# LayerNorm scaling in two routed FFNs: from VectorE to GpSimd

## The chip, the cores and the metric

The kernel runs on one core of one Trainium2 chip. The metric is the device time of one execution in microseconds (us). Engines are named as the profile names them: PE is TensorE's matmul (PEld its weight load), DVE is VectorE, ACT is ScalarE, POOL is GpSimd, SP is SyncE, which here only starts DMAs.

## What is computed

The input is x of shape (2, 4096, 512) in float32: two sequences of 4096 tokens. A block of the model is an FFN, an attention and the same FFN again, each on the LayerNorm of x and each added to x:

```
x = x + 0.5 * ffn(layernorm(x))
x = x + attn(layernorm(x))
x = x + 0.5 * ffn(layernorm(x))

def _layernorm(x, axis=-1, eps=1e-05):
    m = jnp.mean(x, axis=axis, keepdims=True)
    v = jnp.var(x, axis=axis, keepdims=True)
    return (x - m) / jnp.sqrt(v + eps)
```

The FFN is a routing over 64 slots. Every token gets 64 logits from a hidden layer of 256 (gelu), keeps the 8 largest, and their softmax is its weight `alpha` on the slots. The slots gather the tokens with these weights, a GRU cell changes them, and each token reads the slots back with the same weights:

```
h = gelu(ctx @ w1.T + b1);  route_logits = (h @ w2.T + b2) / (abs(tau) + 0.1)
topk_vals, topk_idx = top_k(route_logits, 8);  topk_w = softmax(topk_vals)
slot_input = einsum('bts,btd->bsd', alpha, x);  slot_wsum = alpha.sum(axis=1) + 1e-08
... GRU of slot_input / slot_wsum, linear map wv ...
out = einsum('bts,bsd->btd', alpha, slot_values) @ wo.T + bo
```

The attention is a gated delta rule over 16 heads of 32, with a scan over the tokens. It is not touched here.

## The kernel before

The work is cut into 32 blocks. A block is 128 tokens of both sequences, so one tile of 128 partitions by 2 x 512. The program has five stages one after another: the routing of the first FFN, its GRU, the attention (with the first FFN's read-back in it), the routing of the second FFN, and then its GRU and read-back, which writes the output.

A routing (`ffn_a_phase`, L309) goes over groups of four blocks, with a group of one at the beginning and groups of two and one at the end (`split_blocks`, L53), ten groups in all. Each group passes through six generators. `a_load` starts the DMAs of the token tiles on SP. `a_stats` (L355) takes bn_stats (L361) and bn_aggr (L362) of each half tile on DVE, and the root and reciprocal for the scale (L365 on ACT, L366 on DVE). `a_norm` (L368) makes the normalized tile `xn` (L379, two instructions a block), casts it to float16 on ACT (`xh`, L383), and takes the rest of the split, `xl = xn - xh`, on POOL (L385). PE then transposes both (L394), ACT and DVE copy the transposes from PSUM (L397, L399). `a_hidden` does the hidden layer in three float16 matmuls (`mm3`, L128 to L130), gelu on ACT (L417) and the logits on PE (L421). `a_topk` (L425) is a sequence on DVE for a whole group: L431, the eight largest (L436), their removal (L439), L441, the exponential on ACT (L442), L444, L447, L448, L451, and the split of `alpha` (L457, L458); POOL adds `alpha` to a running sum, `wacc` (L461). `a_slots` transposes `alpha` (L472, L475) and adds up the slots on PE (L482 to L484), reading `xh` and `xl` from the buffers of L380 and L381.

The buffers around the change: `xn` has 2 in each FFN (`CFG`, `XN`), so a block's scaling reuses the buffer of the block two before, which L383 and L385 must have read. `xh` and `xl` have 10 in the first FFN and 11 in the second (`XH`). The first routing has work besides: the weights of the attention are scaled and split (`setup_attention`, L253, with L158, L159, L176 and L177), and a part of the GRU is done ahead (`setup_gh`, L231, L248).

`run_merged` (L60) draws the generators' pieces in the order of their due times (`PA`, L1079), and outside the attention the framework's scheduler then sets the order of each engine's queue. So an instruction that changes its engine can shift others. The attention runs under a written order (`PIPE`, L1081, within `manual_schedule`). Every engine works through its queue in order; a waiting instruction holds all that stand behind it. GpSimd's queue holds, in a routing, only L385, L461, a memset and the last sums of `wacc` (L338).

Of the kernel before, what the change touches and what calls it, by code (L numbers as in the profile page):

```python
# [14 lines left out]
ALU = mybir.AluOpType  # L15
# [79 lines left out]
def tile_macaron(  # L95
# [7 lines left out]
    nc = tc.nc  # L103
    V = nc.vector
# [204 lines left out]
    def ffn_a_phase(load, adst, nm, extra, before=None, after=None):  # L309

        with tc.tile_pool(name=f"sl{nm}", bufs=1, space=PSUM) as slp, tc.tile_pool(name=f"gp{nm}", bufs=1) as gp:
# [3 lines left out]
            with tc.tile_pool(name=f"f{nm}", bufs=2) as wp, tc.tile_pool(name=f"fs{nm}", bufs=2) as sm, \  # L315
                    tc.tile_pool(name=f"ft{nm}", bufs=3, space=PSUM) as ptr, \
                    tc.tile_pool(name=f"fp{nm}", bufs=2, space=PSUM) as ppj, \
                    tc.tile_pool(name=f"fl{nm}", bufs=2, space=PSUM) as ppl:
                groups = split_blocks(NBLK)
                ng = len(groups)  # L320
                pools = (wp, sm, ptr, ppj, ppl)
                st = [dict() for _ in range(ng)]
                items = []
                for g, (b0, n) in enumerate(groups):
                    args = (st[g], nm, g, (b0, n), pools)
                    t0, t1 = b0 / GB, (b0 + n) / GB
                    items += [
                        (t0 - PA["ld"] - n / GB, t1 - PA["ld"] - n / GB, lambda a=args: a_load(*a, load)),
                        (t0 - PA["st"], t0 - PA["st"] + PA["std"], lambda a=args: a_stats(*a)),
                        (t0, t1, lambda a=args: a_norm(*a)),  # L330
                        (t0 + PA["a2"], t1 + PA["a2"], lambda a=args: a_hidden(*a)),
                        (t1 + PA["a2"], t1 + PA["tk"], lambda a=args: a_topk(*a, wacc)),
                        (t1 + PA["tk"], t1 + PA["tk"] + PA["sl"] * n / GB, lambda a=args: a_slots(*a, adst, sl, ng)),
                    ]
                items += extra(gp, ptr, gw, NBLK / GB)
                run_merged(items)
                for i in range(1, GB):
                    nc.gpsimd.tensor_tensor(wacc[:, 0:NB], wacc[:, 0:NB], wacc[:, NB * i:NB * i + NB], ALU.add)  # L338
# [29 lines left out]
    def a_norm(d, nm, gi, blocks, pools):  # L368

        wp, sm, ptr, ppj, ppl = pools  # L370
        mv, rs = d["mv"], d["rs"]
        d["xhl"], d["xT"] = [], []
        for j in range(blocks[1]):
            u = f"{nm}{gi}_{j}"
            xs = d["x"][j]
            xn = wp.tile([P, NB, D], F32, tag="xn", name=f"fxn{u}", bufs=CFG[nm]["XN"])
            for b in range(NB):
                i = NB * j + b
                V.tensor_scalar(xn[:, b], xs[:, b], mv[:, i, 0:1], rs[:, i:i + 1], ALU.subtract, ALU.mult)  # L379
            xh = wp.tile([P, NB, D], F16, tag="xh16", name=f"xh{u}", bufs=CFG[nm]["XH"])  # L380
            xl = wp.tile([P, NB, D], F16, tag="xl16", name=f"xl{u}", bufs=CFG[nm]["XH"])  # L381
            d["xhl"].append((xh, xl))
            nc.scalar.copy(xh, xn)  # L383
            yield (j + 0.2) / blocks[1]
            nc.gpsimd.tensor_tensor(xl, xn, xh, ALU.subtract)  # L385
            yield (j + 0.4) / blocks[1]
            xTh = wp.tile([P, KC, NB * P], F16, tag="xTh", name=f"fxTh{u}", bufs=3)
            xTl = wp.tile([P, KC, NB * P], F16, tag="xTl", name=f"fxTl{u}", bufs=3)
            d["xT"].append((xTh, xTl))
            for src16, dst, eng in ((xh, xTh, 0), (xl, xTl, 1)):  # L390
                pt = ptr.tile([P, KC, NB * P], F16, tag="tr", name=f"fpt{u}_{eng}")
                for k in range(KC):
                    for b in range(NB):
                        nc.tensor.transpose(pt[:, k, b * P:(b + 1) * P], src16[:, b, k * P:(k + 1) * P], ident16)  # L394
                    yield (j + 0.4 + 0.3 * eng + 0.07 * (k + 1)) / blocks[1]
                if eng == 0:
                    nc.scalar.copy(dst, pt)  # L397
                else:
                    V.tensor_copy(dst, pt)  # L399
                yield (j + 0.7 + 0.3 * eng) / blocks[1]  # L400
# [751 lines left out]
```

## Time and profile before

| | |
|---|---|
| Median of 3 runs | 2361.86 us (2361.6 to 2366.88) |
| The profiled execution, its own time | 2367.99 us |
| Its span, first to last instruction | 2366.2 us |
| Mean granted TensorE clock | 0.952 |
| Busy share of the span | PE 89%, PEld 67%, DVE 81%, ACT 48%, POOL 34% |
| First routing, about | 20 to 262 us |
| Second routing, about | 2036 to 2262 us |

A row of the profile's groups gives the line, the engine, the operation, the tiles written and read, their sizes, the count, the busy time in us, the mean of one in ns, and the idle time of the engine just before them with what ended it. The shares above are means over stages with different limits, so the stages are read apart. Tile names end in the FFN's letter: `fxna` is `xn` in the first, `fxnc` in the second. `kx` and `xt` are both token tiles of the second FFN (14 of 32 are kept in SBUF for the read-back).

### The profile page before, as it was taken

Reading aid. Unit: us, or ns where it says so; the run is one execution under the profiler, and the core shown is the slowest. Engines: PE = TensorE matmul, PEld = TensorE weight load, DVE = VectorE, ACT = ScalarE, POOL = GpSimd, SP = SyncE. Lnnn points to the kernel's source line nnn. Section 1 sums busy time; section 2 is a strip of 40 time slices with the busy share of each in tenths; the row PEclk is TensorE's granted clock in tenths of the full one; section 3 lists DMA queues with packets and bytes.
Section 4 is the critical chain, followed back from the end, with each engine's and each line's share of the span. In section 5 each row is a group of like instructions: output and inputs, shape, how many; then the busy total and the mean of one; then the engine's idle time right before and its main releaser. Section 6 shows DMA issues by size and latency. Waiting matters only on the chain.

```text
span 2366.2 us, 101086 instructions
## 1 busy us (share of the span) xinstructions
PE 2113.8 (89%) x44989; PEld 1595.9 (67%) x44989; DVE 1920.3 (81%) x4876; ACT 1134.2 (48%) x1924; POOL 807.7 (34%) x750
## 2 busy tenths in 40 slices
PE   5778879999999999999999999999999976588985
PEld 5667847767777676766767677777667754477863
DVE  7898547988888888888888888888888885797664
ACT  4677445544445444444544444554444521467620
POOL 3333114433334333334434333433333441244200
PEclk9998889999999999999999999999999987789986
DMA  6332323344434344443334344344334332621069
GB/s 215 117 126 90 94 85 130 117 134 130 147 125 129 123 135 131 136 136 116 124 126 140 127 142 135 124 128 138 122 125 147 100 91 69 234 97 59 22 238 342
DMA packets 185444, 310.10 MB, mean 131 GB/s; under 512 B 28976, under 2 KB 82736, under 8 KB 185008
## 3 DMA queue, kind: packets, MB, share of 16 engines
q1 hardware_dynamic: 167600, 260.12, 33.1%
q10 hardware_dynamic: 17408, 43.52, 5.6%
q8 instruction: 352, 5.77, 1.2%
q14 instruction: 84, 0.69, 0.1%
HBM read 192.38 MB, written 111.20 MB: 128 GB/s over the span
## 4 chain that ended last, share of the span: by engine, by line
PE 57%; DVE 13%; DMA 10%; issue 3%; ACT 1%; SPq 1%; POOL 1%; DVEq 0%; ACTq 0%; POOLq 0%
PE apo L1064 9%; PE pa L943 5%; PE pv L128 5%; PE pc L1019 5%; DMA kd<-qk 4%; PE pc L1002 4%; PE pv L129 4%; PE pv L130 4%; PE pq L128 4%; PE pq L129 3%; PE pq L130 3%; PE pc L1012 3%; DMA x1r<-x1d 3%; PE kqt L853 2%; DVE fxnc L379 1%
## 5 line engine op out<-in xcount | busy, mean ns | idle before, releaser
L1064 PE MATMUL apo<-wo,Gt 128*128 128x512 f32 x512 | 281.1, 634 | 28.4 <-DVE x1r L1067 28.3
L128 PE MATMUL pv<-xTh,wgh 128*128 128x256 f16 x1024 | 282.3, 276 | 0.1
L129 PE MATMUL pv<-xTh,wgl 128*128 128x256 f16 x1024 | 280.4, 274 | 0.4 <-issue 0.4
L130 PE MATMUL pv<-xTl,wgh 128*128 128x256 f16 x1024 | 280.5, 274 | 0.0
L998 POOL TENSOR_TENSOR ps<-ST,AC 128x256 f32<-128x256 f32 x128 | 105.4, 823 | 457.2 <-DVE ST L1022 457.0
L128 PE MATMUL pq<-wqh,xTh 128*128 128x384 f16 (+1 forms) x768 | 243.4, 317 | 1.6 <-issue 0.9
L129 PE MATMUL pq<-wqh,xTl 128*128 128x384 f16 (+1 forms) x768 | 241.4, 314 | 0.2 <-DVE xTl L802 0.2
L130 PE MATMUL pq<-wql,xTh 128*128 128x384 f16 (+1 forms) x768 | 241.3, 314 | 0.0
L846 POOL TENSOR_TENSOR qk<-qk,rn 128x512 f32<-128x512 f32 x128 | 138.0, 1079 | 232.9 <-issue 107.3
L820 ACT ACTIVATE qk<-pq,iscA 128x384 f32<-128x384 f32 (+1 forms) x192 | 105.2, 548 | 164.4 <-PE pq L130 141.5
L964 POOL TENSOR_TENSOR KQ<-KQ,Ax 128x512 f32<-128x512 f32 x128 | 168.1, 1313 | 0.8 <-PE pa L943 0.8
L748 DVE TENSOR_TENSOR tmp<-N,MT 128x256 f32<-128x256 f32 (+7 forms) x384 | 162.3, 429 | 5.6
L742 DVE TENSOR_TENSOR tmp<-N,U 128x256 f32<-128x256 f32 (+7 forms) x384 | 164.7, 436 | 1.4
L822 ACT ACTIVATE sq<-pq,iscA 128x384 f32<-128x384 f32 (+1 forms) x192 | 164.8, 858 | 0.0
L1002 PEld LDWEIGHTS pc<-KQ,S 32*32 32x32 f32 x8192 | 123.5, 106 | 51.5 <-ACT Y L1028 31.4
L744 DVE TENSOR_REDUCE MT<-tmp 128x32 f32<-128x256 f32 (+7 forms) x384 | 153.6, 407 | 0.0
L943 PE MATMUL pa<-KQ 32*32 32x64 f32 x8192 | 143.4, 217 | 11.1 <-ACT KQ L856 5.0
L1002 PE MATMUL pc<-KQ,S 32*32 32x64 f32 x8192 | 142.8, 217 | 9.9 <-DVE S L1024 4.5
L1019 PEld LDWEIGHTS pc<-X,u 32*32 32x32 f32 x8192 | 121.9, 106 | 38.2 <-issue 21.1
L1019 PE MATMUL pc<-X,u 32*32 32x64 f32 x8192 | 143.1, 218 | 4.8 <-ACT u L1016 3.5
L943 PEld LDWEIGHTS pa<-KQ 32*32 32x32 f32 x8192 | 121.8, 106 | 37.6 <-issue 14.7
L750 DVE TENSOR_REDUCE N<-tmp 128x32 f32<-128x128 f32 (+4 forms) x320 | 135.3, 423 | 0.0
(303 smaller groups left out, 5728.7 us busy)
## 6 DMA issues: line engine op xcount, KB each, us to landing
d<-a0d ACTq DMA_DIRECT2D x32, 528.0 KB
Ax<-a0d ACTq DMA_DIRECT2D x32, 528.0 KB
xt<-in_x_dram SPq DMA_DIRECT2D x32, 512.0 KB
x<-in_x_dram SPq DMA_DIRECT2D x64, 256.0 KB
x1d<-x SPq DMA_DIRECT2D x64, 256.0 KB
vtd<-vg SPq DMA_DIRECT2D x64, 256.0 KB
kd<-qk SPq DMA_DIRECT2D x64, 256.0 KB
XK<-kd SPq DMA_DIRECT2D x256, 64.0 KB
```

Source lines behind the costliest of these rows:

```text
L128: nc.tensor.matmul(po, lh, rh, start=start, stop=False, skip_group_check=True)
L129: nc.tensor.matmul(po, ll, rh, start=False, stop=False, skip_group_check=True)
L130: nc.tensor.matmul(po, lh, rl, start=False, stop=stop, skip_group_check=True)
L742: V.tensor_tensor(tv, vw(f, o10 + j0, [[C, n], [0, h], [1, ni]]), vw(U, ou + j0 * 17, [[0, n], [16, h], [1, ni]]), ALU.mult)
L744: yield lambda tv=tv, j0=j0: V.tensor_reduce(vw(mt, n * j0, [[1, n], [n, h]]), tv, AX.X, ALU.add)
L748: V.tensor_tensor(tv, vw(f, o11 + r0 * C, [[C, h], [0, n], [1, nk]]), vw(mt, 0, [[0, h], [n, n], [1, nk]]), ALU.mult)
L822: nc.scalar.activation(sq[:, f0:f1].rearrange("p (q g e) -> p q e g", g=NG, e=C), pq[:, 0:f1 - f0].rearrange("p (q e g) -> p q e g", g=NG, ...
L943: nc.tensor.matmul(pa[s, m], KQ[s, 0, c, b, g], KQ[s, :, c, b, g], start=(m == 0), stop=True, skip_group_check=True, tile_position=(32 * q ...
L964: nc.gpsimd.tensor_tensor(kc, kc, bass.AP(Ax.tensor, Ax[:, :, c].offset, [list(a[0]), [1, 2], list(a[1]), [1, C]]), ALU.mult)
L1002: nc.tensor.matmul(pcv[s, b, g, 0:2 * C], S[s, b, g], KQ[s, :, c, b, g], start=(g == 0), stop=False, skip_group_check=True, tile_position=tp)
L1019: nc.tensor.matmul(pcv[s, b, g, C:3 * C], u[s, b, g], d["X"][s, :, m], start=False, stop=True, skip_group_check=True, tile_position=tp)
L1064: nc.tensor.matmul(po, Gt[:, k, b], wo[:, k], start=(k == 0), stop=(k == KC - 1))
```

## The change

The scaling of L379 is issued on GpSimd (`nc.gpsimd`) and no longer on VectorE (`V`). Its operands, its count (64 in each FFN) and everything else stay.

```
             for b in range(NB):
                 i = NB * j + b
-                V.tensor_scalar(xn[:, b], xs[:, b], mv[:, i, 0:1], rs[:, i:i + 1], ALU.subtract, ALU.mult)
+                nc.gpsimd.tensor_scalar(xn[:, b], xs[:, b], mv[:, i, 0:1], rs[:, i:i + 1], ALU.subtract, ALU.mult)
```

One instruction reads a 128 x 512 float32 half tile and, for each partition, a mean and a scale, and writes (x - mean) x scale.

## The prediction

> **What bounds the kernel now.** I first cut the span into stages with the table of busy time by stretch. The edit touches two: the routing of the first FFN (20 to 262 us) and of the second (2036 to 2262 us). Attention, nearly 1700 us between them, holds no edited line and keeps its order.
>
> ```profile
> core 0: us, PE busy (x) PEld busy (x) DVE busy (x) ACT busy (x) POOL busy (x), PEclk, DMA share, GB/s
> 20.00:262.00 242.00, 194.02 (x2260) 173.79 (x2261) 210.10 (x551) 160.97 (x226) 81.02 (x40) 0.92 0.35 114
> 2036.00:2262.00 226.00, 192.26 (x2369) 172.00 (x2369) 181.16 (x502) 153.27 (x212) 81.57 (x45) 0.90 0.25 87
> ```
>
> VectorE is busy 210 of 242 us (87%) and 181 of 226 us (80%), GpSimd only 81 in each. PE's busy time counts overlapping matmuls, so its need is worked out below. Next, the chain of waits within 2020 to 2366 us; its opening line is:
>
> ```profile
> by line: DVE fxnc L379 9.2%; DVE stc L361 8.2%; DMA out_dram<-cxt 4.8%; DVE ahlc L457 4.5%; issue 3.5%; DMA caT<-ald 3.3%; PE plc L421 3.2%; POOL xlc L385 3.2%; DVE fxTlc L399 3.2%; DVE repc L439 3.2%; DMA cxt<-x2d 3.1%; DVE cxt L625 2.9%;
> ```
>
> The edited line leads: 9.2% of 346 us is 32 us on the path that sets the end, and most other entries of the routing are VectorE's too. In the first FFN the chain cannot be followed that far back; there I argue from the 87%. Third, the rows of the operations concerned, from the answers on their lines and the list of groups (count, minimum, median and maximum ns; or busy us, mean ns, idle time before):
>
> ```profile
> L379 DVE TENSOR_SCALAR fxna<-xt,mva,rsa x64: 507/536/2350, 24.1 to 231.9; 128x512 f32<-128x512 f32 x64
> L385 POOL TENSOR_TENSOR xla<-fxna,xha x32: 2119/2132/2574, 26.4 to 247.2; 128x1024 f16<-128x1024 f32 x32
> L457 DVE CAST ahlc<-alc x20: 195/870/2207, 2062.5 to 2259.0; 128x256 f16<-128x256 f32 x14, 128x64 f16<-128x64 f32 x4, 128x128 f16<-128x128 f32 x2
> ...
> L460 POOL MEMSET wacca<- 128x512 f32 x1 | 0.5, 524 | 0.0
> L846 POOL TENSOR_TENSOR qk<-qk,rn 128x512 f32<-128x512 f32 x128 | 138.0, 1079 | 232.9 <-issue 107.3 <-DVE rn L839 81.4 <-ACT x L794 24.3
> L964 POOL TENSOR_TENSOR KQ<-KQ,Ax 128x512 f32<-128x512 f32 x128 | 168.1, 1313 | 0.8 <-PE pa L943 0.8
> L461 POOL TENSOR_TENSOR wacca<-wacca,ala 128x512 f32<-128x512 f32 x7 | 11.0, 1574 | 57.3 <-DVE ala L451 34.0 <-DVE mva L362 23.3
> L379 DVE TENSOR_SCALAR fxna<-xt,mva,rsa 128x512 f32<-128x512 f32 x64 | 45.3, 735 | 5.2 <-POOL xla L385 5.2
> L379 DVE TENSOR_SCALAR fxnc<-xt,mvc,rsc 128x512 f32<-128x512 f32 x36 | 25.3, 736 | 5.3 <-POOL xlc L385 5.3
> L379 DVE TENSOR_SCALAR fxnc<-kx,mvc,rsc 128x512 f32<-128x512 f32 x28 | 20.6, 760 | 8.7 <-POOL xlc L385 8.7
> ```
>
> The scaling has a median of 536 ns but a mean of 735, and its worst case, 2350 ns, is its own time plus most of one L385: now and then it stands behind GpSimd.
>
> **The change, part by part.**
>
> *Removed from VectorE.* 64 instructions a routing: 45.3 us in the first, 25.3 + 20.6 = 45.9 in the second. Back to back, VectorE's instructions overlap by about 0.08 us (two of L379 in a row took 0.99 us), so 64 x 0.08 = 5 us come off: about **40 us freed in each**.
>
> *Added to GpSimd.* No row shows this operation there. Nearest below: the L460 memset of the same 128x512, 524 ns, which reads nothing. Nearest above: the two-input L846 of that size, 1079 ns; the far end is L964, 1313 ns. One input beside none costs 288 ns against 204 at 128x128 (cast L136, memset L138), and 524 x 1.41 = 740. I take **0.8 us**, half way between 524 and 1079, and keep 0.52 to 1.31. That is 64 x 0.8 = 51 us more per routing (33 to 84): GpSimd goes from 81 to some 132 us. Per block it does L385 2.13 us, two scalings 1.6, and L461's share of about 0.35, in all 4.1 us (up to 5.1 at the far end), where a block now takes 226/32 = 7.1 us. It becomes the bound only if one scaling exceeds (7.1 - 2.13 - 0.35)/2 = 2.3 us.
>
> The Trainium skill's "GPSIMD Engine Reference" (section 4.1, Engine selection) speaks against the edit: elementwise work belongs on VectorE, GpSimd being about twice as slow on two inputs, though roughly at line rate on one. Its section 3.1 gives 769 ns for 512 elements in a tight loop; by that the addition would be 49 us instead of 51. No run here shows a one-input row of this size.
>
> *Dearer on VectorE: the port.* Against its plainest repetition each of these operations now loses time. First routing: L441 7 x (947 - 679), L451 7 x (920 - 674), L457 14 x (774 - 294), L177 16 x (850 - 429, from L748 of the same size) and 8 x (859 - 737): some 18 us. Second: L457 14 x (1019 - 294) and 4 x (821 - 195), L458 14 x (688 - 411), L441, L444 and L451 about 6 together: some 23 us. If waits follow GpSimd's busy time (132/81), they grow by 63%, 11 to 15 us; if they follow the summed squares of its instructions, since short ones are waited for briefly ((2.13² + 2 x 0.8²)/2.13² = 1.28), by 5 to 6 us. I take **8 us**, between the two. VectorE's net relief is 40 - 8 = 32 us a routing.
>
> The skill's "SBUF — State Buffer" (section Who interferes with whom) says that a VectorE instruction in a two-port mode, or with two SBUF inputs, and a GpSimd instruction that reads SBUF exclude each other for a whole instruction. The maxima above (2350, 2207) agree; L1006, with one input in PSUM, never exceeds 426 ns. But the 768 two-input products of the inverse (L742, L748) average 436 and 429 ns beside GpSimd, so blocking is not met on every encounter. By the page, charged on every encounter, the sum would take some 14 us in place of the 8.
>
> *Waits and queues.* Built, the changed program has all 128 scalings in GpSimd's queue and none in VectorE's. Two xn buffers already made the scaling of block j+2 wait for L385 of block j, so that order is no new wait. New is what stands ahead in the queue: L385 waits for ACT's cast, L461 for the top-k on VectorE; while either waits, the next scaling waits too, and behind it ACT's cast, PE's transposes and the hidden layer. I charge nothing while GpSimd runs at least one block ahead. Without that cover see rival B. ACT loads its tables twice more (2 x 1.28 us), behind other work. SP's loads of the token tiles, the output casts and the weight preparation keep their counts; only their order shifts, and the DMA share is 0.35 and 0.25, so I price that at 0, plus or minus 5 us.
>
> *What is late next.* PE. From a dense stretch of the timeline (start, duration, count):
>
> ```profile
> 247.03 0.27 PE L128 MATMUL fpha<-fxTha,w1h 128*128 128x256 f16 x1
> 247.13 0.27 PE L129 MATMUL fpha<-fxTha,w1l 128*128 128x256 f16 x1
> 247.24 0.27 PE L130 MATMUL fpha<-fxTla,w1h 128*128 128x256 f16 x1
> ...
> 247.68 0.19 PE L482 MATMUL sla<-ahla,xha 128*128 128x64 f16 x1
> 247.71 0.19 PE L483 MATMUL sla<-ahla,xha 128*128 128x64 f16 x1
> ```
>
> Starts lie 0.11 us apart for hidden matmuls, 0.03 for slot matmuls; in the same way 0.055 for transposes and 0.11 for logits. One block: 24 x 0.11 + 24 x 0.03 + 18 x 0.055 + 8 x 0.11 = 5.2 us; 32 blocks 168 us, at the granted clock 168/0.92 = 183 and 168/0.90 = 187 us. The first routing has 96 matmuls of L248 besides, about 10 us. After the edit the loads are, first routing: PE 193, VectorE 178, ACT 164, GpSimd 132; second: PE 187, ACT 154, VectorE 149, GpSimd 133. PE leads in both.
>
> **The sum.** An engine that leads does not run without gaps: VectorE, leading now, fills 87% and 80%. With PE at 87% the stages last 193/0.87 = 222 and 187/0.87 = 215 us: 20 and 11 us less, **31 us** together. With PE at 93% it would be about 60, near the whole relief of 64; with PE at 80% nothing. The profiled execution took 2367.99 us (span 2366.2 and 1.8 around it), 6 us over the median of the runs, 2361.86. On its own time the sum gives 2337 us; taking the same 31 us off the median, I predict **2331 us**.
>
> **Rivals.**
> - *A, the relief goes nowhere* (within 7 us): PE, its clock or ACT paces the blocks anyway. For it: PE already needs 183 of 242 us, the clock in these stages falls to 0.73 in places, and PE waits for ACT's gelu at L421. Against: the chain runs through VectorE until about 2200 us, not through PE. About 2362 us.
> - *B, slower: the scaling is held in GpSimd's queue.* Now GpSimd idles 57 us before L461 in the first routing (longest 15.4) and 48 in the second, waiting for VectorE. In the built order the next scalings stand behind L461. Exposed in full that is about 105 us against 64 of relief: 2362 + 41 = 2403 us. It decides from the point where over 60% of that idle time reaches PE. Against: the top-k itself comes earlier on a freer VectorE, and L461 stands two or three blocks ahead of PE.
> - *C, the whole relief counts:* PE closes up to 93% and more; 2362 - 60 = 2302 us.
> - That the edit doesn't do what it says is excluded by the built order.
>
> **How the numbers follow.** Forecast (gains of 7 to 52 us) 0.66; A 0.12; B 0.14; C 0.08. From the measured scatter and the figure asked for, 0.3% (7 us) is about what can be told from no change. Faster = forecast + C = 0.74, same = A = 0.12, slower = B = 0.14. The range reaches from C (2302) to A's upper edge (2369). A scaling at 1.31 us rather than 0.8 takes GpSimd to 165 us, still below PE; the sum of squares rises from 1.28 to 1.76 times, so VectorE waits 9 to 11 us more a routing, and the relief of 64 falls to some 44, still above the 31. Left out are most of B and a part of C, under 2 in 10.
>
> **What would show it.** Right: L379 on GpSimd at 0.5 to 1.3 us; VectorE's busy time in the two routings at about 178 and 149 us; the routings about 20 and 11 us shorter; L457 and L451 with higher means; attention unchanged. Wrong: ACT's cast waiting long for fxn on GpSimd, with L461 ahead of it (B); PE busier but at a lower clock (A); L379 above 2.3 us.

## The result, and the profile after

The changed kernel takes **2434.11 us** (median of 4 runs, 2426.58 to 2442.05) beside 2361.73 of the kernel before on the same chip: ratio **1.0299** [1.0277, 1.0321]. That is 72 us slower, where 31 us faster was forecast, and outside the forecast's range. The profiled execution took 2442.05 us (span 2440.3).

First, where the time went. From the first statistics to the last slot sum, the first routing of the kernel before lasts 260 us and the second 235; measured in the same way they now last 286 and 285. The rest of the span (attention 1751 us, tail 103) is shorter by 3 us. The table of busy time by stretch over these two routings, first of the kernel before, then of the changed kernel:

```profile
core 0: us, PE busy (x) PEld busy (x) DVE busy (x) ACT busy (x) POOL busy (x), PEclk, DMA share, GB/s
16.00:276.00 260.00, 205.20 (x2472) 184.11 (x2472) 221.73 (x596) 170.43 (x242) 83.56 (x45) 0.92 0.35 114
2027.00:2262.00 235.00, 192.26 (x2369) 172.00 (x2369) 189.36 (x526) 154.29 (x214) 81.57 (x45) 0.88 0.28 96
```

```profile
16.00:302.00 286.00, 213.58 (x2470) 190.39 (x2470) 186.18 (x532) 172.55 (x243) 219.88 (x109) 0.88 0.32 104
2053.00:2338.00 285.00, 206.75 (x2369) 182.66 (x2370) 147.32 (x462) 156.57 (x215) 215.66 (x109) 0.83 0.23 78
```

VectorE was relieved as meant: 186 and 147 us busy, against 222 and 189 before, 78 us less in all (the forecast had 64). But GpSimd went from 84 and 82 to 220 and 216 us, not to the forecast 132. The row of the scaling says why (count, then minimum, median and maximum ns):

```profile
L379 POOL TENSOR_SCALAR fxna<-xt,mva,rsa x64: 2067/2074/2911, 20.4 to 260.6; 128x512 f32<-128x512 f32 x64
L379 POOL TENSOR_SCALAR fxnc<-xt,mvc,rsc x36: 2068/2073/2516, 2056.0 to 2286.4; 128x512 f32<-128x512 f32 x36
L379 POOL TENSOR_SCALAR fxnc<-kx,mvc,rsc x28: 2067/2072/2616, 2069.5 to 2292.7; 128x512 f32<-128x512 f32 x28
```

One scaling takes **2.07 us**, four times VectorE's median of 536 ns, and minimum and median are nearly the same: it is the instruction itself and not a wait inside it. GpSimd now leads. From the first scaling to the last (24 to 232 us and 2034 to 2215 us before; 20 to 263 us and 2056 to 2295 us now), these are the rows of the kernel before and of the changed kernel:

```profile
24.10:232.40 208.30, 167.17 (x1932) 149.85 (x1933) 188.85 (x489) 143.40 (x201) 74.14 (x36) 0.92 0.38 123
2034.50:2215.20 180.70, 151.15 (x1761) 134.74 (x1762) 152.15 (x397) 125.61 (x170) 72.14 (x36) 0.88 0.29 100
```

```profile
20.40:262.70 242.30, 179.72 (x1979) 159.98 (x1979) 159.61 (x445) 149.57 (x207) 210.30 (x100) 0.87 0.34 113
2056.00:2294.80 238.80, 170.56 (x1844) 150.30 (x1845) 118.01 (x371) 132.94 (x177) 205.47 (x101) 0.81 0.24 82
```

VectorE was busy 91 and 84% of that time before; now GpSimd is, at 87 and 86%. The whole loss lies there (34 and 58 us longer); what comes before the first scaling and after the last is 8 us shorter in each routing.

PE was busy 8 and 14 us longer over the routings, at a granted clock of 0.88 and 0.83 (0.92 and 0.88 before), which is the sign that rival A named. But it fills less of them, 75 and 73% against 79 and 82%, so PE is not what paces them. No run separates what the lower clock costs from the rest.

The opening line of the chain of waits within 2060 to 2345 us:

```profile
by line: POOL fxnc L379 12.4%; issue 8.9%; PE plc L421 5.0%; POOL xlc L385 4.5%; DVE ahlc L457 3.4%; PE fphc L130 2.9%; PE fphc L129 2.7%; PE fphc L128 2.6%; PE fptc L394 2.4%; ACT hTc L417 2.3%; DVE ahlc L458 2.1%; PE pgc L531 1.7%; DVE al
```

The same instruction still leads, now on POOL. And from the list of waits in the second routing (who waited for whom: us in total, times, longest):

```profile
ACT xhc L383 <- POOL fxnc L379: 52.3, 16, 6.1
POOL waccc L461 <- DVE alc L451: 48.2, 7, 21.6
...
DVE stc L361 <- DMA xt<-x2d: 43.1, 11, 9.8
...
DVE mvc L362 <- POOL fxnc L379: 29.3, 7, 10.9
```

The rows of the kernel before for two of these:

```profile
ACT xhc L383 <- DVE fxnc L379: 6.4, 4, 2.9
DVE stc L361 <- DMA xt<-x2d: 8.8, 1, 8.8
```

ACT's cast waited 6.4 us for the scaling before; now 52.3. VectorE waits for token tiles that GpSimd frees late (SP, which starts the loads, waits 119 us for the scaling, 63 before), and, which was not foreseen, for the small buffers of the statistics until GpSimd has read them.

### The profile page after: what moved, and what is told of

The parts are those of the page before. It is cut to its first block, busy times and chain, and to the rows that moved or that the text cites. A ratio compares the mean times of both kernels' runs of the same rounds, so it can differ in the third digit from the quotient of the medians.

```text
span 2440.3 us, 101121 instructions
## 1 busy us (share of the span) xinstructions
PE 2133.3 (87%) x44989; PEld 1609.3 (66%) x44989; DVE 1842.7 (76%) x4748; ACT 1139.2 (47%) x1926; POOL 1078.0 (44%) x878
## 5 line engine op out<-in xcount | busy, mean ns | idle before, releaser
L379 POOL TENSOR_SCALAR fxna<-xt,mva,rsa 128x512 f32<-128x512 f32 x64 | 138.1, 2168 | 25.1 <-DVE rsa L366 21.1
```

What stands on the lines that cost most here:

```text
L379: nc.gpsimd.tensor_scalar(xn[:, b], xs[:, b], mv[:, i, 0:1], rs[:, i:i + 1], ALU.subtract, ALU.mult)
```

## The experiments

Three theories stood at the start. *Price*: a scaling costs GpSimd 2.07 us whatever runs beside it, and GpSimd's 32 x (2.13 + 2 x 2.07 + 0.35) = 212 us a routing set the pace. *Contention*: 2.07 us is a cheaper instruction held up by VectorE. *Queue* (the forecast's rival B): scalings stand behind L461 and L385 in GpSimd's queue. Later a second question came up: what the relief of VectorE is worth by itself. Every ratio is to the kernel before, run on the same chip, and comes with its 95% interval; that kernel's median was 2361 to 2366 us throughout.

**The price by itself.** At the end of the kernel before, where VectorE has nothing to do, GpSimd runs each of these forms four times: `nc.gpsimd.tensor_scalar(y5, x5, m_, s_, ALU.subtract, ALU.mult)` as in the change, other sizes, one operation instead of two, constants, a copy, products.

> The kernel before, with rows added behind its end: on GpSimd alone, four each of the scaling as it stands (128x512, two operations, a mean and a scale per partition), of half and of double its length, of one operation instead of two, of constants instead of per-partition scalars, of a copy, of a product with a broadcast scale, of a product of two tiles, of a float16 output, of a memset. Price theory (the instruction itself is dear): the scaling takes 2.0 to 2.1 us here as well, with nothing beside it, about half and double at half and double length, and a product with a broadcast scale 1.0 to 1.1 us. Contention theory (the 2.07 us come from sharing with VectorE): it takes 0.5 to 1.1 us here.

The groups of the probe (busy us, mean ns, idle before): twice the size, as in the change, one operation, product of two tiles, product with a broadcast column, copy.

```profile
L644 POOL TENSOR_SCALAR py<-px,pm__40506 128x1024 f32<-128x1024 f32 x4 | 15.1, 3778 | 0.4
L640 POOL TENSOR_SCALAR py<-px,pm__40506 128x512 f32<-128x512 f32 x4 | 8.3, 2074 | 0.1
...
L646 POOL TENSOR_SCALAR py<-px,pm__40506 128x512 f32<-128x512 f32 x4 | 6.3, 1563 | 0.4
...
L656 POOL TENSOR_TENSOR py<-px 128x512 f32<-128x512 f32 x4 | 5.0, 1262 | 0.3
...
L654 POOL TENSOR_TENSOR py<-px,pm__40506 128x512 f32<-128x512 f32 x4 | 4.2, 1038 | 0.3
L652 POOL COPY py<-px 128x512 f32<-128x512 f32 x4 | 2.4, 612 | 0.2
```

With nothing beside it the scaling takes the same 2074 ns. Contention as the cause of the price falls. The form is dear, not the bytes: a copy of the same tile takes 612 ns and even a product of two tiles 1262.

**Cheaper work in the same place.** GpSimd keeps all the scalings, in forms of other prices. e2 and e5 leave the subtraction of the mean out; e6 neither subtracts nor scales, and its copies do not wait for the statistics.

```
e2: nc.gpsimd.tensor_tensor(xn[:, b], xs[:, b], bc(rs[:, i], 1, D), ALU.mult)            # 1.04 us
e5: nc.gpsimd.tensor_scalar(xn[:, b], xs[:, b], rs[:, i:i + 1], None, ALU.mult)          # 1.56 us
e6: nc.gpsimd.tensor_copy(xn[:, b], xs[:, b])                                            # 0.61 us
```

> All 128 scalings on GpSimd, but as a product of the token tile with the broadcast scale; the mean is not subtracted, so the kernel leaves out that part of the computation. Price theory: 1.05 to 1.1 us each (as L846), GpSimd needs 2.13 + 2.16 + 0.35 = 4.6 us a block instead of 6.6 and no longer paces; the time falls below the kernel before, 2310 to 2350 us. Queue theory (rival B: the scaling is held behind L385 and L461, whatever it costs): still slower than before, 2380 to 2420 us.

> All 128 scalings on GpSimd as one multiplication by the per-partition scale, 1563 ns each as measured alone; the subtraction of the mean is left out. Knee theory (GpSimd costs nothing until its need a block, 2.13 + 0.35 + 2T, reaches that of the other engines, about 5.8 us): 5.6 us, just below the knee, 2362 to 2380 us. Loop theory (the scaling's length adds to a loop that every block or group passes through, whatever the engine's load): on the line through 1.04 us (2363) and 2.07 us (2434), so about 2398, 2388 to 2410 us.

> All 128 scalings replaced by a copy on GpSimd, 612 ns each as measured alone; the scaling and the subtraction are left out. Knee theory: as the broadcast product, 2355 to 2365 us, since GpSimd had stopped pacing there. Loop theory: about 30 us lower than at 1.04 us, 2325 to 2342 us.

Measured: e6 2320.1 us, 0.9808 [0.9785, 0.9831]; e2 2362.64, 0.9985 [0.9966, 1.0003]; e5 2373.82, 1.0041 [1.0018, 1.0064]; and the change itself, at 2.07 us, 1.0299. e2 lies between the ranges of its two theories, e5 where the knee theory had it, e6 below both of its ranges. So the price decides the sign, softly: from 1.56 to 2.07 us, 128 x 0.51 = 65 us more work cost 60 us; from 1.04 to 1.56 it was 11 us. The routings, with 260 and 235 us before, take 255 and 241 in e2, 255 and 248 in e5: the second pays first. And e2 says that a price within the forecast's own bounds (0.52 to 1.31) was no surety: at 1.04 us, as a product, the move gains nothing.

**Half of the work, or the other half.** e3 scales only the second tile of each block on GpSimd; e4 moves the scaling to GpSimd and in exchange the subtraction L385 to VectorE.

```
e3: (nc.gpsimd if b else V).tensor_scalar(xn[:, b], xs[:, b], mv[:, i, 0:1], ...)
e4: nc.gpsimd.tensor_scalar(...)  and  V.tensor_tensor(xl, xn, xh, ALU.subtract)
```

> Only the second sequence's scaling (b = 1) on GpSimd, the first stays on VectorE. Price theory: GpSimd needs 2.13 + 2.07 + 0.35 = 4.55 us a block, below the 7.1 us of a block before, and VectorE is freed of 20 us a routing: 2335 to 2360 us. Queue theory: each block still waits for a scaling in GpSimd's queue: 2375 to 2420 us.

> All scalings on GpSimd, and in return L385 (xl = xn - xh) on VectorE. Price theory: GpSimd needs 4.15 + 0.35 = 4.5 us a block and does not pace; VectorE gives up 40 us a routing and takes 32 x 1.1 = 35 us: about the kernel before, 2345 to 2385 us. Queue theory: L385's wait for ACT is gone from GpSimd's queue, L461's is not; some way between the two kernels, 2385 to 2420 us.

Measured: e3 2382.55 us, 1.0070 [1.0038, 1.0102]; e4 2388.16, 1.0115 [1.0071, 1.0159]. Half the scalings cost a quarter of the loss. Both lie where the queue theory had them; the control below bears on that. e4 takes GpSimd down to 158 and 152 us busy in the routings and is still slower than before: L385 costs VectorE 1.22 us a block, which is most of what the two scalings took from it.

**What the relief is worth.** e7 has no scaling at all: `xn = xs` (nothing subtracted or scaled, two token buffers more), but its cast no longer waits for the statistics. e9 puts that wait back by letting ACT's cast carry a scale (one for both tiles of a block, mean left out):

```
e9: nc.scalar.activation(xh, xn, AF.Identity, bias=0.0, scale=rs[:, NB * j:NB * j + 1])
```

> VectorE's relief alone: the scaling is left out on all engines, ACT's cast and L385 read the token tile itself, and the room of the two xn buffers goes to two more token tiles in each routing; GpSimd keeps only L385 and L461. If the relief of 32 us a routing that the forecast counted is worth half its size or more: 2300 to 2335 us. If VectorE's load was not what the routings waited for: 2345 to 2365 us.

> The relief run again, with the wait on the statistics put back: no engine scales the tiles in a pass of its own (mean subtraction left out; the cast to 16 bits on ScalarE carries one scale of the block, so both tiles of a block get the first one's), but the cast now has to wait for the finished statistics, as the scaling did. Theory one, VectorE's 40 us a routing are what the runs without scaling gained: 2310 to 2330, like them (2316). Theory two, they gained because the work no longer waited for the statistics, and VectorE's hours are not the bound: 2345 to 2365.

Measured: e7 2316.28 us, 0.9787 [0.9755, 0.9819]; e9 2330.05, 0.9870 [0.9840, 0.9900]. The routings of e9, by stretch:

```profile
16.00:257.00 241.00, 202.40 (x2472) 182.29 (x2472) 185.70 (x533) 175.54 (x244) 81.02 (x45) 0.92 0.36 123
1996.00:2225.00 229.00, 190.70 (x2370) 171.18 (x2370) 148.96 (x462) 160.18 (x216) 81.17 (x45) 0.90 0.28 99
```

VectorE is down to 186 and 149 us busy, GpSimd is where it was, and the routings are 19 and 6 us shorter. e7 lies in its first range, e9 at the upper end of its first. The 33 us by e9's median (31 by its ratio), beside the forecast's 31, are not VectorE's relief alone: e9 also has two token buffers more in each routing, and no pass of its own between the statistics and the cast.

**GpSimd's load alone.** The kernel before, with the same 64 scalings a routing added on GpSimd into a tile that nobody reads.

```
+            xd = wp.tile([P, NB, D], F32, tag="xd", name=f"fxd{u}", bufs=1)
+                nc.gpsimd.tensor_scalar(xd[:, b], xs[:, b], mv[:, i, 0:1], rs[:, i:i + 1], ALU.subtract, ALU.mult)
```

> The kernel before, VectorE still scaling, and GpSimd given the same 64 scalings a routing as dummies into a buffer that nobody reads (132 us more of GpSimd work a routing at 2.07 us each). Theory one, GpSimd's load is what makes the changed kernel slow, since the subtraction behind it in GpSimd's queue is late: 2415 to 2450, as slow as the changed kernel or slower. Theory two, what is slow is that the cast on ScalarE waits for a scaling that GpSimd starts late: here the cast has VectorE's result, so 2362 to 2390.

Measured: 2524.56 us, 1.0677 [1.0638, 1.0716], above both expectations, and on the side of the first. The row of VectorE's scaling in the first routing (L387 is the old L385):

```profile
L380 DVE TENSOR_SCALAR fxna<-xt,mva,rsa 128x512 f32<-128x512 f32 x64 | 51.3, 822 | 83.6 <-POOL xla L387 83.6
```

VectorE idles 84 us (5 before) for the two `xn` buffers, which the late subtraction on GpSimd holds. A busy GpSimd thus hurts through L385 even when nobody waits for its extra work, and more than in the changed kernel, where the scaling shares L385's queue and VectorE needs no `xn` buffer.

**Late token tiles; ScalarE instead.** e8 is e2 with six token buffers instead of four in the second routing (`XT=6`). e12 scales the second tile of each block on ScalarE, as one activation with `bias=nb[:, i:i + 1], scale=rs[:, i:i + 1]`.

> The broadcast product on GpSimd (as in the second experiment, without the mean) and six token buffers instead of four in the second routing, where bn_stats waited 24 us for loads into buffers that the scaling on GpSimd frees late. If those loads are what keeps the second routing from gaining: 10 to 25 us below the second experiment, 2338 to 2353 us. If they only fill other waits: within 6 us of it, 2357 to 2368 us.

> The scaling of the second tile of each block on ScalarE, as one activation with the scale and the bias of the token, and the first on VectorE as before; GpSimd is left as in the kernel before. VectorE is relieved of 20 us a routing, ScalarE gets 32 activations of 128x512, some 25 us. If relief of VectorE is worth its whole size: 2330 to 2345. If relief is absorbed as with the cheap GpSimd scaling: 2355 to 2368. If ScalarE is late next: above 2368.

Measured: e8 2359.55 us, 0.9986 [0.9971, 1.0002], so two more token buffers bring e2 no gain; e12 2363.41, 1.0001 [0.9978, 1.0024]: 0.82 us each on ScalarE, and no gain either.

**GpSimd's queue.** e11 is the changed kernel with the sum L461 on VectorE (`V.tensor_tensor(wacc...)`), so that no scaling stands behind a sum that waits for the top-k. e14 does the same to e2. e15 and e16 add buffers to e14 and e11: four instead of two for the statistics (`bufs=4` at L359 and L364) and `XT=6`. e13 is e6 with a read of the group's scales on GpSimd ahead of the copies.

> The changed kernel with one edit: the sum of the gate weights (L461), which holds GpSimd's queue until VectorE has ended a block's top-k, goes to VectorE, so that scalings never stand behind it. Price theory (GpSimd's 212 us of work a routing set the pace): 2420 to 2435, no more than the few us of the sum itself. Queue theory (scalings wait behind the held sum): 2385 to 2410.

> The copies of 0.61 us in the place of the scaling (neither subtracted nor scaled), but now GpSimd first reads the group's finished scales into a small tile, so that its copies wait for the statistics as the scaling does; without that wait the copies gave 2320. Price theory (the time rises with what GpSimd does between statistics and cast, from 2330 at nothing to 2363 at 1.04 us): 2340 to 2355. Wait theory (GpSimd's in-order wait for the statistics costs the gain, whatever the price): 2358 to 2370. Neither: 2320 to 2335, and then the 1.04 us run lost its gain to its own two-input instruction, which makes VectorE's port waits 8 to 12 us a routing longer.

> The 1.04 us scaling (mean left out) with the gate weights' sum L461 on VectorE, so that no scaling stands behind a sum that waits for the top-k. If the held sum is what takes the gain: 2335 to 2350. If it isn't: 2357 to 2367.

> The same, and also four buffers instead of one rotation for the statistics' small tiles, and six token buffers instead of four in the second routing. If queue order and buffers together take the gain: 2330 to 2345, as with a free scaling. If what takes it is the scaling's own time between statistics and cast, and VectorE's port waits: 2352 to 2365.

> The changed kernel with the same three edits (sum L461 on VectorE, buffers for the statistics, six token buffers): what is left is GpSimd's work, 206 us of a routing of 270 to 278 with the sum moved alone (2417). If GpSimd's work sets the pace: 2400 to 2418. If its waits do: 2365 to 2395.

Measured: e11 2416.89 us, 1.0226 [1.0199, 1.0254]; e13 2328.54, 0.9856 [0.9825, 0.9888]; e14 2347.07, 0.9939 [0.9915, 0.9963]; e15 2340.95, 0.9905 [0.9880, 0.9930]; e16 2396.66, 1.0149 [1.0128, 1.0170]. e13 settles less than it was meant to: its trace has copies ahead of the read of their scales (the first copy at 15.1 us, the first read at 22.6), so the wait was put back only in part; its time is in the last of its three ranges. e14 and e15 fell where the queue theory had them; e11 and e16 fell between the ranges of the two theories, e16 with half of the loss gone. That looked like the queue, and needed a control.

**The control, and a faster kernel.** e17 makes the same three edits (the sum below, `bufs=4` for the statistics, `XT=6`) in the kernel before; e18 makes them in the half version e3.

```
-        nc.gpsimd.tensor_tensor(wacc[:, 0:n], wacc[:, 0:n], al, ALU.add)
+        V.tensor_tensor(wacc[:, 0:n], wacc[:, 0:n], al, ALU.add)
```

> The kernel before, scaling on VectorE, with the three edits of e15 and e16 (sum L461 on VectorE, four buffers for the statistics, six token buffers in the second routing). If the edits end waits that only scalings on GpSimd bring: 2358 to 2372, as before or a little slower, since VectorE gets the sums. If they help any kernel: 2335 to 2350, and e15 and e16 prove nothing on GpSimd's queue.

> The second tile of each block scaled on GpSimd (2.07 us), the first on VectorE, the whole computation kept, with the same three edits; without them it took 2383. GpSimd's work a routing is as in the 1.04 us kernel, which came to 2341 with the edits. If GpSimd's held queue was what the half version lost to: 2340 to 2358, faster than the kernel before. If it lost to the subtraction on GpSimd coming later and VectorE waiting for its buffer (61 us in the second routing): 2365 to 2383.

Measured: **e17 2332.93 us, 0.9858 [0.9842, 0.9875]**, the whole computation kept, just below the second expectation and faster than both kernels; e18 2356.16, 0.9953 [0.9937, 0.9969], in the queue theory's range. The edits help the kernel before as much as the changed one (and e2 and e3 less), so e11, e14 to e16 and e18 are no evidence for the queue theory. With the edits on both sides, the change costs 1.0149/0.9858 = 1.0295, without them 1.0299: the same 3%, each known to about 0.3%. ACT's cast waits for the scaling in e16 as in the change, 45 and 47 us in the two routings, though L461 has left GpSimd's queue. The half version costs 1.0096 (1.0070 without), the scaling at 1.04 us 1.0048. The stretches of e16 (two lines) and of e17:

```profile
16.00:286.00 270.00, 201.85 (x2472) 181.17 (x2472) 182.95 (x542) 172.36 (x243) 207.25 (x99) 0.92 0.33 110
2029.00:2292.00 263.00, 198.82 (x2370) 175.43 (x2370) 146.97 (x472) 153.83 (x213) 205.78 (x99) 0.86 0.24 85
```

```profile
16.00:259.00 243.00, 195.88 (x2471) 176.61 (x2472) 214.21 (x606) 172.41 (x244) 70.34 (x35) 0.96 0.37 122
2010.00:2232.00 222.00, 186.20 (x2370) 168.16 (x2370) 177.21 (x536) 150.71 (x211) 70.94 (x35) 0.92 0.29 101
```

With the held sum gone and L362's wait for the statistics' buffers down from 52 to 7 us, GpSimd is busy 201 of the 234 us and 200 of the 218 us from the first scaling to the last (86 and 92%), and the changed routings stay 27 and 41 us longer than e17's. That leaves GpSimd's work, rather than its wait for the top-k, as what sets their pace. A further thing is to be seen in e17: VectorE does ten more instructions a routing and is busy 8 and 12 us *less* than before (222 and 189).

## Why the prediction was wrong, step by step

1. *VectorE leads both routings, and 40 us a routing of its work can go*: right, and more than that went (78 us in all against 64 net). The deduction of 8 us a routing for port waits (VectorE's instructions that run longer beside GpSimd's) was too much. The five operations of the top-k that lose time to the port (L441, L444, L451, L457, L458) took 41 + 52 us before and 44 + 49 after, the same, although GpSimd was busy 2.6 times as long.
2. *A scaling on GpSimd costs 0.8 us, at most 1.31*: **this step failed.** It measured 2.07 us, alone (e1) as in the kernel. The bounds came from a memset and from products of two tiles of the same size; both are other forms of instruction, and a smaller form was taken as a floor and a larger one as a ceiling only because of their counts of inputs. GpSimd's addition was 133 us a routing, not 51. The Trainium skill's "GPSIMD Engine Reference" gives 769 ns for 512 elements (section 3.1) and calls one-input work roughly line-rate (4.1, Engine selection); the copy at 612 ns fits that, the two-operation scaling does not, and the measurement decides.
3. *GpSimd is the bound only if a scaling exceeds 2.3 us*: failed too, and would have misled even with the right price, since 2.07 lies below 2.3. The 7.1 us a block had the beginning and the end of the routing in them; from the first scaling to the last, a block took 208/32 = 6.5 us in the first routing and 181/32 = 5.6 in the second. And the step let GpSimd fill them entirely, while further on PE was allowed 87%; GpSimd reached 86% in the change. With both, the limit is an estimate of (0.86 x 6.5 - 2.13 - 0.35)/2 = 1.6 us in the first routing and (0.86 x 5.6 - 2.13 - 0.35)/2 = 1.2 us in the second. e5 at 1.56 us agrees: its first routing is 5 us shorter than before, its second 13 us longer.
4. *New waits at nothing while GpSimd runs a block ahead*: the condition did not hold. ACT's cast waits 52 us for the scaling in the second routing and 36 in the first. It goes with the price: at 1.04 us (e2) it is 13 and 14 us, against 6 and 9 before. So this follows from step 2. Missed altogether was the wait of L362 on the statistics' buffers (22 and 29 us).
5. *PE is late next, at 87%: 31 us of gain*: near in size where the scaling costs nothing: e9 gained 33 us (19 and 6 in the routings, where 20 and 11 were forecast), but with the other differences named above, so the match may be luck. Not shown is that PE, or VectorE's relief, is the reason: e17 gains as much while it leaves the scalings on VectorE, and e12, which takes half of them off it, gains nothing.
6. *The range stays inside at 1.31 us*: wrong. At 1.04 us e2 gained nothing. Where the some 30 us between it and e9 went is shown only in part: the five port-bound operations took 52 + 64 us in e2, 45 + 52 in e9, so its own two-input products cost VectorE some 19 us.

Rival B had the right sign and place (the cast waits for a scaling held on GpSimd) but the wrong cause. Its price came from the idle time before L461, and with L461 out of that queue, and the buffers of e17, the change's loss is the same: 3% either way.

Still open: which of e17's three edits brings its 33 us, why half the scalings (e3, e18) cost anything, the part of the lower clock, and the part of e2's missing gain that the port waits do not cover. An e9 with the edits of e17, which would tell whether VectorE's relief is worth anything more there, was not run.

## What to carry to other kernels

Before an elementwise instruction is moved to GpSimd, time that very form (operation count, scalar operands) there: rows of another form at the same shape say little about it. Set the limit for an engine that takes over a step by the time a block takes while blocks are under way (here 5.6 and 6.5 us, not 7.1), and at the share that the leading engine reaches there (84 to 91%), not at 100%. And when an edit repairs part of a loss, run the same edit in the kernel before: here the repair was worth as much there.

## What the runs showed of the hardware

GpSimd's tensor_scalar on 128 partitions took 1219, 2074 and 3778 ns for 256, 512 and 1024 elements, so 3.3 ns an element on 0.37 us. At 512 the second operation costs 0.51 us (2074 against 1563). VectorE took 0.54 us for the same work.

Which instruction GpSimd ran mattered more to VectorE than how long it ran. With tensor_scalars (e5, the change) the port-bound operations stayed at 93 us in the two routings together; with products (e2) they rose to 116. The second routing of e2, and of e13 with copies in their place (its L460 is L458):

```profile
L458 DVE TENSOR_TENSOR ahlc<-alc,ahlc 128x256 f16<-128x256 f32 x14 | 13.5, 1005 | 0.0
```

```profile
L460 DVE TENSOR_TENSOR ahlc<-alc,ahlc 128x256 f16<-128x256 f32 x14 | 6.0, 470 | 0.0
```

The Trainium skill's "SBUF — State Buffer" (Who interferes with whom) has a VectorE instruction with two SBUF inputs contend with a GpSimd instruction that reads SBUF, for an exclusive lock on the ports that they share; e2 agrees, and the tensor_scalars, which read SBUF as well, do not. L458 reads two tiles in SBUF and takes 411 to 414 ns with nothing on GpSimd beside it. In the trace of the change, ten of its 28 largest (128 x 256) ran beside scalings alone: nine took 410 to 413 ns, one 824. In e2 six ran beside products alone: five took 1255 to 1258 ns. In e13 few met a copy (23 of 28 met nothing), but the two that ran beside one took 824 ns. The rule does not tell these forms apart.

In e17, with L461 off GpSimd (and the buffers added), the cast L457 falls from a mean of 1019 ns in the second routing to 372, and L461 itself takes 0.68 us instead of 1.3:

```profile
L461 DVE TENSOR_TENSOR waccc<-waccc,alc 128x512 f32<-128x512 f32 x7 | 4.8, 679 | 0.0
L457 DVE CAST ahlc<-alc 128x256 f16<-128x256 f32 x14 | 4.7, 372 | 0.1
```

L461 begins on GpSimd when `alpha` is ready (L451), which is when VectorE begins L457. In the kernel before, 15 of the 28 largest casts of the two routings ran beside L461 alone and took 809 ns on average; the six with nothing on GpSimd beside them took 283. VectorE's busy time did not rise where it took the sums over: from the change to e11, where L461 alone was moved, it fell by 0 and 1 us in the two routings, from e2 to e14 by 3 and 5. So the short sum on the other engine cost VectorE in waits as much as it costs when VectorE does it, or more.
